# Half-empty taps of a 3x3 convolution as 64x64 quarters, in a fixed order with the neighbour layer in slots

## The chip, the cores and the metric

The kernel runs on one core of a Trainium2 chip. The engines that matter are TensorE (PE, matrix products), VectorE (DVE), ScalarE (ACT), GpSimd (POOL) and SyncE (SP, which here only issues DMAs). Each engine works through its own queue of instructions in order, and engines wait for each other by semaphores. DMAs are issued from a queue of SP or ACT, and an issue that has to wait holds what stands behind it in that queue. The metric is the device time of one execution in microseconds; fewer is better.

## The reference, cut to what matters

The network has four layers on an input `x` of 8 images, 64 channels, 128x128 pixels, in float32. Each layer adds its result to its input:

```python
x = x + _L0_conv_ref(_gn(x), ...)   # deformable convolution
x = x + _L1_conv_ref(_gn(x), L1_conv_weight)   # 3x3 convolution, 64 -> 64 channels, padding 1
x = x + _L2_conv_ref(_gn(x), ...)   # scans along rows and columns
x = x + _L3_conv_ref(_gn(x), ...)   # nearest neighbours ("neighbour layer"), see below
```

`_gn` is a group norm over pairs of channels of an image. Layer 1, the one that is changed, is a plain convolution:

```python
return jax.lax.conv_general_dilated(x, weight, window_strides=(1, 1),
    padding=[(PAD, PAD), (PAD, PAD)], dimension_numbers=('NCHW', 'OIHW', 'NCHW'))
```

Layer 3 shrinks the image by a 4x4 convolution with stride 4 to 32x32, looks for every pixel for the nine of its 7x7 surroundings that differ most, averages them, runs a second 3x3 convolution over both, scales by an attention value, and resizes to 128x128 bilinearly. Its pieces run beside layer 1.

## The kernel before, in words

**Layout.** Two images make a pair, so that 2 x 64 channels fill 128 partitions; there are four pairs. Layer 0 is done for all pairs first. `Net.rest` then takes the pairs one after the other: `conv3x3` (layer 1), `scan_layer` (layer 2), and `neighbours` (layer 3). `neighbours` is a generator: it is cut into pieces by `yield`, and the generator of pair p is handed as `aside` to the `conv3x3` of pair p+1, which draws pieces from it. Pair 0 has no pieces beside it; the pieces of pair 3 run alone at the end. Two large tiles in SBUF (`room`) change roles from pair to pair.

**The convolution** (`conv3x3`, from L603). Sixteen *fills* (L624 to L630) bring the normed image into the other room in a form for products with 128 rows of contraction: ACT norms 8 image rows into a tile `nx` (two buffers), and SP issues four DMAs that put even image rows on partitions 64 to 127 and odd image rows, moved by one, on partitions 0 to 63, for both images. At one position of this room a product thus reads two image rows that follow each other. A tap pair `m` covers two of the rows that an output row needs; the three kernel rows need two such pairs, and one of the two is half empty: for even output rows (`e` = 0) the pair `m` = 1 has weights on partitions 0 to 63 alone, for odd ones (`e` = 1) the pair `m` = 0 has them on 64 to 127 alone. The other halves of the weights are zeros (memset at L615). For 8 output rows (a *row block*) and each parity `e`, 12 products (3 shifts `dx`, 2 tap pairs `m`, 2 images `i`) go into one bank of PSUM: image 0 to partitions 0 to 63, image 1 to 64 to 127 (L632 to L641). As data are float32, each product is two matmul instructions in the program, the low and then the high part of the weights. VectorE adds the bank to the residual (L643), and takes statistics for the next norm (`bn_stats`, L647). The tag `b` has two buffers in PSUM.

**The neighbour layer's pieces**, 46 in number (from L976):
- one for weights and norm factors (`quarter`: loads from ACT's queue, L988 and L990, 32 tiny products, L996),
- eight for the 4x4 convolution (loads of 1 MB in four issues on ACT's queue, L1010, two blocks ahead; 32 instructions, L1018; ACT empties them, L1019),
- two for transposes, the write to DRAM (L1033) and the loads back (L1035, L1044),
- sixteen for distances and maxima (`farthest`, L1137 to L1153, one product and ten VectorE instructions; `means` of the piece before: transposes L1162, copy by ACT L1164, products L1167),
- two for the second 3x3 convolution (its weights loaded by SP, L1072, L1073; L1086, L1087),
- one for attention and a widened image (L1090 to L1103),
- sixteen for the upsampling, two for each of eight tiles: the first loads a tile of the residual by SP (`up_x`, two buffers, L1109) and interpolates along rows (ACT L1116, VectorE L1117), the second does eight additions on VectorE (L1125, L1126) and issues the store by SP (L1127).

**What sets the order.** In this region the framework's scheduler orders each engine's queue from its own estimate of when things are ready; program order is a priority. Pieces are drawn at three places per row block, one piece each. It can so move a load ahead of a store that stands before it in the program, or a piece's loads ahead of the convolution. The scan layers before and after are written in an order of their own (`manual_schedule`), which the scheduler leaves as it is.

Of the kernel before, what the change touches and what calls it, by code (L numbers as in the profile page):

```python
# [9 lines left out]
F32 = mybir.dt.float32  # L10
# [6 lines left out]
P = 128  # L17
C = 64
H = 128
# [23 lines left out]
class Net:  # L43
# [559 lines left out]
    def conv3x3(self, p, a, room, r, nb, aside):  # L603

        nc, src = self.nc, self.ins["l1_w"]
        st = self.small.tile([P, NCH, 6], F32, tag="st", name=f"gn2_st{p}")
        two = room.rearrange("p (i n w) -> p i n w", i=2, w=H)  # L610
        half = [slice(0, C), slice(C, P)]
        with self.tc.tile_pool(name=f"b_conv{p}", bufs=1) as cp, self.tc.tile_pool(name=f"b_conv2_{p}", bufs=2) as wp:

            w = cp.tile([P, 2, 2, 3, C], F32, name=f"l1_w{p}")
            nc.gpsimd.memset(w, 0.0)  # L615
            for e in range(2):
                for n in range(2):
                    for h in range(2):
                        dy = 2 * n - 1 + h - e
                        if abs(dy) < 2:  # L620
                            nc.scalar.dma_start(w[half[h], e, n], src[:, 3 * dy + 3 : 3 * dy + 6, :])
            nc.gpsimd.memset(two[half[0], :, 0, :], 0.0)
            nc.gpsimd.memset(two[half[1], :, H // 2, :], 0.0)
            for n in range(16):  # L624
                t = wp.tile([P, 2, 4, H], F32, tag="t", name=f"nx{p}_{n}")
                rows = a[:, 8 * n : 8 * n + 8, :].rearrange("p (m e) w -> p e m w", e=2)
                nc.scalar.activation(t, rows, AF.Identity, bias=nb, scale=r)
                for i in range(2):
                    nc.sync.dma_start(two[half[1], i, 4 * n : 4 * n + 4, :], t[half[i], 0])
                    nc.sync.dma_start(two[half[0], i, 4 * n + 1 : 4 * n + 5, :], t[half[i], 1])  # L630
            for n in range(0, H // 2, 4):
                for e in range(2):  # L632
                    po = self.ps.tile([P, 4, H], F32, tag="b", name=f"c1_{p}_{n}_{e}")
                    calls = []
                    for dx in (0, -1, 1):
                        c0, c1 = max(0, -dx), min(H, H - dx)
                        for m in range(2):
                            for i in range(2):
                                calls.append((po[half[i], :, c0:c1], w[:, e, m, dx + 1], two[:, i, n + m : n + m + 4, c0 + dx : c1 + dx]))
                    for k, (o, lt, mv) in enumerate(calls):  # L640
                        nc.tensor.matmul(o, lhsT=lt, rhs=mv, start=k < 2, stop=k >= len(calls) - 2)  # L641
                    rows = a[:, 2 * n : 2 * n + 8, :].rearrange("p (m e) w -> p e m w", e=2)[:, e]
                    nc.vector.tensor_add(rows, rows, po)  # L643
                    next(aside, None)
                for k in range(2):
                    g = n // 2 + k
                    nc.vector.bn_stats(st[:, g, :], a[:, 4 * g : 4 * g + 4, :].rearrange("p h w -> p (h w)"))  # L647
                next(aside, None)
            for _ in aside:
                pass  # L650
        return self.groupnorm(self.small, self.ps1, "small", st, "gn2")


# [517 lines left out]
class Scan:  # L1171
# [106 lines left out]
    def products(self, g, h, py, fx, xs, first):  # L1278

        om = self.outs.rearrange("p (n c) -> p n c", c=P)  # L1280
        calls = [(om[:, T + 1 + h - k], fx[:, :, k, :]) for k in (h, 1 - h)] if fx is not None else []
        calls += [(om[:, 2 * f + h], x) for f, x in xs]
        if py is None:
            py = self.net.ps.tile([P, 2, NB], F32, tag="y", name=self.name("py", h, g))
        for n, (lt, mv) in enumerate(calls):
            self.nc.tensor.matmul(py, lhsT=lt, rhs=mv, start=first and n == 0, stop=n == len(calls) - 1 and (fx is not None))  # L1286
        return py
# [387 lines left out]
```

## Time and profile before

| | us |
|---|---|
| median of 3 runs | 15756.33 (15753.49 to 15758.31) |
| the profiled execution | 15728.88, its span 15727.1 |
| convolution, pair 0: first fill to next stage's L1376 | 11733.0 to 11912.1 |
| pair 1, with pieces: the same | 12608.8 to 12889.9 |
| pair 2 | 13588.1 to 13869.5 |
| pair 3 | 14570.4 to 14852.4 |

Times within the execution count from the start of the span. An engine's busy time in a stretch says whether it is full there; matmuls overlap, so a PE that is busy throughout can still be loaded in steps of different length. A line such as `SPq` shows what an engine's queue issued and when; for DMAs it is the issue, not the transfer. `x3072` counts instructions, and the number behind the bar is the time in which at least one of the group ran.

### The profile page before, as it was taken

How to read it: one execution, taken by the hardware profiler on the slowest of the kernel's cores; microseconds unless marked ns; L12 is line 12 of the kernel's file. 1: busy time of each engine (PE TensorE's matmuls, PEld its weight loads, DVE VectorE, ACT ScalarE, POOL GpSimd, SP SyncE). 2: the span in 40 equal slices, each digit the busy share in tenths (PEclk: the TensorE clock that was granted, in tenths of full speed). 3: DMA queues.
4: the chain of work that ended last, by engine and by line, in shares of the span. 5: the costliest groups of instructions: out<-in, count | busy, mean ns of one | idle time of the engine just before them, and what ended most of it. 6: DMA issues, size and time to landing. Idle time of an engine off the chain costs nothing. (4 is left out here: it accounts for less than half of the span.)

```text
span 15727.1 us, 121681 instructions
## 1 busy us (share of the span) xinstructions
PE 10293.3 (65%) x32760; PEld 3736.6 (24%) x32760; DVE 11824.0 (75%) x27353; ACT 3233.2 (21%) x5498; POOL 10294.7 (65%) x10572
## 2 busy tenths in 40 slices
PE   7864577447755553776556655564338888888886
PEld 2211122112211111221111111111114444434443
DVE  6777777777777777777777777777766958779587
ACT  1100111001100000110000000000015637456373
POOL 5777777777777777777777777777753605336052
PEclk9986698669977775988778887787569999999998
DMA  5444444345533333543333333333342443534434
GB/s 174 125 122 134 131 149 155 115 121 157 156 118 117 115 115 111 157 138 120 113 116 115 115 120 115 115 115 108 108 141 71 122 120 98 133 117 123 118 92 114
DMA packets 901297, 1933.56 MB, mean 123 GB/s; under 512 B 200060, under 2 KB 436996, under 8 KB 877572
## 3 DMA queue, kind: packets, MB, share of 16 engines
q0 software_dynamic: 442368, 1208.55, 26.2%
q1 hardware_dynamic: 383200, 679.50, 14.2%
q10 hardware_dynamic: 75044, 37.72, 1.2%
q8 instruction: 265, 4.34, 0.1%
q14 instruction: 420, 3.44, 0.1%
HBM read 1540.74 MB, written 208.10 MB: 111 GB/s over the span
## 5 line engine op out<-in xcount | busy, mean ns | idle before, releaser
L380 POOL DMA_INDIRECT g<-table,idx x9216 | 8716.7, 946 | 2822.5 <-issue 2636.4
L391 DVE TENSOR_TENSOR g<-g,corner_weights 128x256 f32<-128x256 f32 x9216 | 3778.1, 416 | 2699.9 <-DMA g<-table,idx 2660.2
L392 DVE TENSOR_REDUCE sm<-g 128x64 f32<-128x256 f32 x9216 | 5016.9, 580 | 9.0
L292 PE MATMUL po<-xe,wt 128*54 128x512 f32 (+3 forms) x8384 | 4292.6, 627 | 13.6 <-ACT ob L302 13.0
L398 PE MATMUL sp<-ident,sm 128*128 128x128 f32 x4096 | 1536.4, 380 | 4169.7 <-DVE sm L392 4154.4
L403 ACT COPY s<-sp 128x512 f32<-128x512 f32 x1024 | 598.8, 585 | 8695.4 <-PE sp L398 8695.2
L398 PEld LDWEIGHTS sp<-ident,sm 128*128 128x128 f32 x4096 | 629.8, 155 | 6730.5 <-DVE sm L392 5062.0
L292 PEld LDWEIGHTS po<-xe,wt 128*54 128x54 f32 x8384 | 901.5, 132 | 1341.4 <-issue 1059.8
L409 PE MATMUL yp<-s,wd 128*64 128x512 f32 (+1 forms) x2560 | 903.2, 713 | 25.4 <-ACT s L403 24.8
L1433 POOL COPY l_yb<-ln_y 128x512 f32<-128x512 f32 x128 | 87.9, 718 | 1242.0 <-ACT room L1413 1128.0
L641 PE MATMUL c<-room,l_w 128*64 128x508 f32 (+1 forms) x3072 | 737.9, 605 | 43.1 <-DMA room<-nx 28.3
L1209 ACT ACTIVATE fx<-room,ln_b,ln_g 128x512 f32<-128x512 f32 x512 | 654.2, 1304 | 89.1 <-DMA in<-fx 80.1
L1225 PE MATMUL pv<-in,tabs 128*128 128x512 f32 x1024 | 555.4, 669 | 98.1 <-DMA in<-fx 47.0
L1286 PE MATMUL py<-in,outs 128*128 128x512 f32 x1024 | 520.3, 633 | 2.4 <-ACT ms L1313 2.4
L1286 PE MATMUL py<-x,outs 128*128 128x512 f32 x1024 | 476.2, 600 | 0.0
L1324 POOL TENSOR_TENSOR ms<-ms,ln_y 128x512 f32<-128x512 f32 x256 | 268.4, 1059 | 271.2 <-DVE ln_y L122 266.6
L1259 DVE TENSOR_TENSOR_SCAN z<-tabs,z,uu 128x256 f32<-128x256 f32 x512 | 407.5, 837 | 27.0 <-POOL uu L1475 26.3
L1303 PE MATMUL pc<-mix,h 64*128 64x128 f32 x4096 | 314.7, 295 | 138.2 <-DVE h L1568 96.5
L641 PEld LDWEIGHTS c<-room,l_w 128*64 128x64 f32 x3072 | 293.4, 139 | 377.1 <-issue 309.7
L402 PE MATMUL s<-ident,sm 128*64 128x128 f32 x512 | 176.3, 344 | 300.7 <-DVE sm L392 288.6
L643 DVE TENSOR_TENSOR room<-room,c 128x512 f32<-128x512 f32 x128 | 87.7, 687 | 371.9 <-PE c L641 368.7
L409 PEld LDWEIGHTS yp<-s,wd 128*64 128x64 f32 (+1 forms) x2560 | 261.6, 159 | 433.5 <-issue 317.9
(423 smaller groups left out, 10271.4 us busy)
## 6 DMA issues: line engine op xcount, KB each, us to landing
g<-table,idx POOLq DMA_INDIRECT x9216, 2.7
in<-fx SPq DMA_DIRECT2D x1024, 128.0 KB
xe<-in_x_dram SPq DMA_DIRECT2D x56, 1408.0 KB
table<-q SPq DMA_DIRECT2D x256, 256.0 KB
y<-ys SPq DMA_DIRECT2D x128, 256.0 KB
room<-in_x_dram SPq DMA_DIRECT2D x64, 512.0 KB
room<-nx SPq DMA_DIRECT2D x256, 128.0 KB
back<-z SPq DMA_DIRECT2D x128, 256.0 KB
```

The lines of the kernel that those rows point to most:

```text
L292: nc.tensor.matmul(po[:, r0:r1, c0:c1], lhsT=wt[:, t, :], rhs=xe[:, row + r0 : row + r1, c0 + dx : c1 + dx], start=n == 0, stop=n == len(u ...
L380: nc.gpsimd.indirect_dma_start(out=tq[:, k, :], out_offset=None, in_=flat[i], in_offset=bass.IndirectOffsetOnAxis(ap=idx[:, at : at + 1], ...
L391: nc.vector.tensor_mul(t[:, ks], t[:, ks], w)
L392: nc.vector.tensor_reduce(sm[:, ks], t[:, ks].rearrange("p k q c -> p k c q"), axis=mybir.AxisListType.X, op=ALU.add)
L398: nc.tensor.transpose(sp[:, j, :], sm[:, j * P : (j + 1) * P], self.ident)
L403: nc.scalar.copy(st[i][:, :, m * P : (m + 1) * P], sp)
L409: nc.tensor.matmul(yp[half[i], :], lhsT=wd[rows, j, :], rhs=src[rows, :], start=j == 0, stop=j == 4)
L641: nc.tensor.matmul(o, lhsT=lt, rhs=mv, start=k < 2, stop=k >= len(calls) - 2)
L1209: self.nc.scalar.activation(fx[:, e].rearrange("p h (o m) -> p h o m", m=self.INNER), src, AF.Identity, bias=self.w["ln1_b"], scale=self.w ...
L1225: self.nc.tensor.matmul(pv, lhsT=self.tabs[:, at : at + P], rhs=fx[:, :, h, :], start=h == 0, stop=h == 1)
L1259: self.nc.vector.tensor_tensor_scan(z[:, i, 1 : NB + 1], decay, u[:, i, :], z[:, i, 0:1], ALU.mult, ALU.add)
L1286: self.nc.tensor.matmul(py, lhsT=lt, rhs=mv, start=first and n == 0, stop=n == len(calls) - 1 and (fx is not None))
```

## The change

Three things change in `conv3x3`:

1. The products of half-empty tap pairs no longer read 128 partitions with zeros for weights on half of them. `quarters` reads the 64 partitions that have weights, so that each such product takes a 64x64 quarter of the array. The two parities' quarters of one `dx` are written one after the other: four products (parity 0 or 1, image 0 or 1) that use the four different quarters and two banks. The number of products stays 24 per row block.
2. The order is written out under `manual_schedule`: three fills first; then for each row block `k` the fill `k + 3`, the full products of parity 0, slot, the quarters of both parities, the add of parity 0, slot, the full products of parity 1, its add, the two statistics, slot.
3. Pieces of the neighbour layer are drawn in these 48 slots by a table (`due`): one piece in every second slot up to ten pieces in slot 19, then 36 pieces in the 26 slots from 20 to 45. Whatever a piece issues on any engine, its DMAs on SP and ACT too, keeps its place in program order.

```diff
-            for n in range(16):
+            def fill(n):
                 t = wp.tile([P, 2, 4, H], F32, tag="t", name=f"nx{p}_{n}")
 ...
-            for n in range(0, H // 2, 4):
-                for e in range(2):
-                    po = self.ps.tile([P, 4, H], F32, tag="b", name=f"c1_{p}_{n}_{e}")
 ...
-                        for m in range(2):
-                            for i in range(2):
-                                calls.append((po[half[i], :, c0:c1], w[:, e, m, dx + 1], two[:, i, n + m : n + m + 4, c0 + dx : c1 + dx]))
-                    for k, (o, lt, mv) in enumerate(calls):
-                        nc.tensor.matmul(o, lhsT=lt, rhs=mv, start=k < 2, stop=k >= len(calls) - 2)
 ...
+            def beside(slot):
+                due = (slot + 1) // 2 if slot < 20 else 10 + (slot - 19) * 36 // 26
+                while done[0] < due:
+                    done[0] += 1
                     next(aside, None)
+            def products(po, k, e, m, rows, left):
+                for dx in (0, -1, 1):
+                    c0, c1 = max(0, -dx), min(H, H - dx)
+                    left[e] -= 1
+                    for i in range(2):
+                        mv = two[rows, i, 4 * k + m : 4 * k + m + 4, c0 + dx : c1 + dx]
+                        nc.tensor.matmul(po[e][half[i], :, c0:c1], lhsT=w[rows, e, m, dx + 1], rhs=mv, start=left[e] == 5, stop=left[e] == 0)
+            def quarters(po, k, left):
+                for dx in (0, -1, 1):
+                    c0, c1 = max(0, -dx), min(H, H - dx)
+                    for e in range(2):
+                        left[e] -= 1
+                        for i in range(2):
+                            mv = two[half[e], i, 4 * k + 1 - e : 4 * k + 5 - e, c0 + dx : c1 + dx]
+                            nc.tensor.matmul(po[e][half[i], :, c0:c1], lhsT=w[half[e], e, 1 - e, dx + 1], rhs=mv, start=left[e] == 5, stop=left[e] == 0)
 ...
+            with self.tc.manual_schedule():
+                for n in range(3):
+                    fill(n)
+                for k in range(16):
+                    if k + 3 < 16:
+                        fill(k + 3)
+                    po = [self.ps.tile([P, 4, H], F32, tag="b", name=f"c1_{p}_{k}_{e}") for e in range(2)]
+                    left = [6, 6]
+                    products(po, k, 0, 0, slice(0, P), left)
+                    beside(3 * k)
+                    quarters(po, k, left)
+                    add(po, k, 0)
+                    beside(3 * k + 1)
+                    products(po, k, 1, 1, slice(0, P), left)
+                    add(po, k, 1)
+                    for g in (2 * k, 2 * k + 1):
+                        nc.vector.bn_stats(st[:, g, :], a[:, 4 * g : 4 * g + 4, :].rearrange("p h w -> p (h w)"))
+                    beside(3 * k + 2)
+                for _ in aside:
+                    pass
```

More of the change, by code (lines that the diff above doesn't have):

```diff
@@ L630, in conv3x3 @@
                     nc.sync.dma_start(two[half[0], i, 4 * n + 1 : 4 * n + 5, :], t[half[i], 1])
-            for n in range(0, H // 2, 4):
-                for e in range(2):
-                    po = self.ps.tile([P, 4, H], F32, tag="b", name=f"c1_{p}_{n}_{e}")
-                    calls = []
-                    for dx in (0, -1, 1):
-                        c0, c1 = max(0, -dx), min(H, H - dx)
-                        for m in range(2):
-                            for i in range(2):
-                                calls.append((po[half[i], :, c0:c1], w[:, e, m, dx + 1], two[:, i, n + m : n + m + 4, c0 + dx : c1 + dx]))
-                    for k, (o, lt, mv) in enumerate(calls):
-                        nc.tensor.matmul(o, lhsT=lt, rhs=mv, start=k < 2, stop=k >= len(calls) - 2)
-                    rows = a[:, 2 * n : 2 * n + 8, :].rearrange("p (m e) w -> p e m w", e=2)[:, e]
-                    nc.vector.tensor_add(rows, rows, po)
-                    next(aside, None)
[L645 to L648, printed above, removed]
@@ L649, in conv3x3 @@
-            for _ in aside:
-                pass
+            done = [0]
+            def beside(slot):
+                due = (slot + 1) // 2 if slot < 20 else 10 + (slot - 19) * 36 // 26
+                while done[0] < due:
+                    done[0] += 1
+                    next(aside, None)
+            def products(po, k, e, m, rows, left):
[5 more added lines that the diff above has]
+                        nc.tensor.matmul(po[e][half[i], :, c0:c1], lhsT=w[rows, e, m, dx + 1], rhs=mv, start=left[e] == 5, stop=left[e] == 0)
@@ new lines, in add @@
+            def add(po, k, e):
+                rows = a[:, 8 * k : 8 * k + 8, :].rearrange("p (m e) w -> p e m w", e=2)[:, e]
+                nc.vector.tensor_add(rows, rows, po[e])
+            with self.tc.manual_schedule():
[18 more added lines that the diff above has]
+                    pass
```

## The prediction

> **What bounds the kernel now.** I read the page first (shares, the convolution's group), then busy time by stage, then the convolution's own line by stage, then SyncE's queue in the last of the stages. The page says that no engine is full over the whole span, and that the 3x3 convolution (L641) has 3072 matmul instructions:
>
> ```profile
> span 15727.1 us, 121681 instructions
> ...
> PE 10293.3 (65%) x32760; PEld 3736.6 (24%) x32760; DVE 11824.0 (75%) x27353; ACT 3233.2 (21%) x5498; POOL 10294.7 (65%) x10572
> ...
> L641 PE MATMUL c<-room,l_w 128*64 128x508 f32 (+1 forms) x3072 | 737.9, 605 | 43.1 <-DMA room<-nx 28.3
> ```
>
> The source has 1536 products, so one product is two instructions. The four convolutions lie at 11733 to 11912 us (pair 0, alone), and, with the neighbour layer of the pair before beside them, at 12609, 13588 and 14570 us, 281, 281 and 282 us each from their first fill (ACT, L627) to the next stage's first instruction (L1376). Busy time by stretch, with columns stretch, its length, PE, PEld, DVE, ACT, POOL, granted clock, DMA share and GB/s:
>
> ```profile
> 11733.00:11912.10 179.10, 167.75 (x773) 90.88 (x774) 46.39 (x83) 19.73 (x16) 0.00 (x0) 0.97 0.21 51
> 12608.80:12699.50 90.70, 82.92 (x500) 48.89 (x501) 12.98 (x28) 22.35 (x24) 0.00 (x0) 0.90 0.84 177
> 12699.50:12716.90 17.40, 17.40 (x81) 5.62 (x78) 5.95 (x9) 3.56 (x4) 0.00 (x0) 1.00 0.56 133
> 12716.90:12795.00 78.10, 78.10 (x374) 35.33 (x374) 61.77 (x179) 11.56 (x32) 0.00 (x0) 1.00 0.00 1
> 12795.00:12823.00 28.00, 27.64 (x133) 10.36 (x131) 5.78 (x15) 5.25 (x13) 0.00 (x0) 1.00 0.25 91
> 12823.00:12885.90 62.90, 50.02 (x228) 17.56 (x224) 62.03 (x119) 9.31 (x26) 0.00 (x0) 0.94 0.57 217
> ```
>
> Row one is pair 0: TensorE full, everything else idle. The others are pair 1's stages: the 4x4 convolution (L1018), its hand-over through DRAM, the distances and maxima (L1137 to L1167), the second 3x3 convolution (L1086), and the upsampling (L1117 to L1127). TensorE is full without a hole through all of them but the last, where VectorE is (62.03 of 62.90). So a cheaper convolution pays until 12823, and not after. The convolution's own instructions in pair 0 and in the last stage:
>
> ```profile
> 11733.00:11912.10 179.10, 166.77 (x768) 90.06 (x768) 0.97 0.21 51
> ...
> 12823.00:12885.90 62.90, 48.85 (x224) 16.55 (x220) 0.94 0.57 217
> ```
>
> SyncE's queue in the upsampling, before:
>
> ```profile
> 12814.42 0.80 SPq L1109 DMA_DIRECT2D up_x<-y  x2
> 12828.32 0.34 SPq L1127 DMA_DIRECT2D out_dram<-up_x  x1
> 12832.17 0.32 SPq L1109 DMA_DIRECT2D up_x<-y  x1
> 12835.13 0.34 SPq L1127 DMA_DIRECT2D out_dram<-up_x  x1
> 12839.26 0.32 SPq L1109 DMA_DIRECT2D up_x<-y  x1
> 12843.70 0.34 SPq L1127 DMA_DIRECT2D out_dram<-up_x  x1
> ```
>
> Two loads go out first. Every load is one tile ahead of the store before it, so VectorE never waits for one: stores are 6.8 to 8.7 us apart.
>
> **The change, part by part.** The sum goes against the profiled execution (15728.9 us, span 15727.1); the median of the runs is 27.4 above it, and I add the difference to the median.
>
> *Quarters.* In steady state single starts in the trace come in pairs, one for each column half, a pair every 0.426 us (11800.071, .497, .923). A row block of 8 image rows has 48 instructions, 24 pairs, 10.2 us. After, 24 instructions stay in pairs (12 x 0.426 = 5.12) and 24 become 64x64 tiles. Four of these at once never run in this trace. Two at once is the upper end: 5.12 us, no gain. Four at once is the lower end: 6 x 0.426 = 2.56; less is excluded, since each quarter of the array still streams its 6. The nearest rows are 64x64 products at 5101.629 and 5101.636 (opposite corners, both running) and the row halves of L1303 (13136.000 and .007). Each pair there starts together though the second half of an earlier product is still to come, so I take four.
>
> The row on order: where one bank of pair 0 ends, the instruction that signals VectorE starts at 11801.446, and the first of the next bank, behind it in the program, at 11801.349. The Trainium skill, "TensorE: Matmul & The Clock Gate", section "The mechanism" of Part 3, speaks against the change: matmuls start and end in program order. As each product is two passes on one tile, strict order would let only neighbours overlap, two at a time, the quarters would gain nothing (5.12), and the total would be the last rival's. The trace contradicts it here by those 97 ns.
>
> Changing the tile shape: before the 64x64 products of L409 the step is 0.52 in place of 0.43, and the next 0.48, so 0.15 us per change, 0.30 per row block. A row block is 5.12 + 2.56 + 0.30 = 7.98 us, or three slots of 2.66.
>
> *Pair 0* runs no pieces. Before: 11737.7 to 11904.5, 166.8 us. After: 3.0 (the wait for fills at its start: 166.8 - 384 x 0.4265) + 48 x 2.66 = 130.7. **-36.1 us.** The adds hide: VectorE has 2 x 0.69 + 2 x 0.69 of work in 8. Fills run ahead on ACT, one in 2.6 us against 8 needed.
>
> *The fixed order, pairs 1 to 3.* Now each queue runs as written. From the first fill, pair 1:
> - First product 5.8 (as before, 12614.5). Slots 0 to 17: 18 x 2.66 = 47.9. Eight blocks of L1018 at 3.6 (64 instructions took 7.63 less the last one's tail) = 28.8; L996 1.4.
> - Before, weights and the first loads of the neighbour layer were issued from 12594, ahead of the fills. Now they stand in ACT's queue behind four fills: pair 0's fills end at +9.4, then 8 issues of 0.6, landing about 2 later: +16.3, where TensorE comes at +12.6. A wait of 3.7, with the products of the slot queued behind it. Twelve load issues of 0.65 follow; the first 1 MB lands near +24: 1.4 more, and 1.5 for a cold start. L1018 ends at **90.5**; before, 90.7.
> - Last block to first distance: 12699.95 to 12716.87, 16.9, plus 0.5: **107.9**. Four slots and two transposes cover 12.1 of it; 5.3 is a hole.
> - Distances: TensorE per piece 0.75 (L1137), 0.64 to the copy, 0.53 of copy (L1164), 0.65 (L1167): 2.57, x16 = 41.1. Before, convolution products filled the copy's 0.53; in a fixed order nothing does. 11 slots 29.3. Five slots hold two pieces, whose transposes wait for VectorE's chain of about 3.3 us: 1.1 each, 5.5. **183.8** (before, 186.0 at the load of L1086's weights).
> - Weights of L1086: issue, landing, subtract (12794.8 to 12799.3): 4.4, now bare. Two halves of 7.5, slot 33, then two slots, attention, add, statistics and the first interpolation 9.6: **215.4**; before, 214.2.
>
> So everything the quarters save there (12 row blocks against 11.3, at 2.2 each, some 26 us) goes into holes that the old order did not have.
>
> *Upsampling.* Each piece pair is load, interpolate, then add, store. As written on SyncE that is load 0, store 0, load 1: load 1 stands behind a store that waits for VectorE to finish tile 0. VectorE then lacks tile 1 until store and load, 2 MB, have passed. The two loads at 12814.42 (2 MB) moved until 12820.9: 6.4 us. Lower end: a load alone, 3.9; upper, store and load in turn, 3.9 + 4.85 (the chain's last load) = 8.7. I take 6.4, the same bytes. Interpolation (2.0) and the convolution's VectorE work hide in it. Eight additions are 4.83, so a cycle is 11.3 against some 8.3 before: 7 x 11.3 + 4.83 = 83.9, plus 2.0 for the last fill's four DMAs between store 0 and load 1. 85.9 against 62.9: **+23.0**.
>
> *End.* Two adds and two statistics now come after the last addition: 2.4, then the norm, 5.5 (pair 0: 11906.6 to 11912.1). Before, this lay beside the last store: 4.0. **+3.9.**
>
> Pair: 215.4 + 85.9 + 7.9 = 309.2 against 281.1: +28.1. Three: +84.3. With pair 0: **+48.2**: 15777 for the profiled execution, **15805** for the median.
>
> **The rivals.**
> - *Not slower: the load is not late.* If x tiles land within VectorE's other work, the upsampling stays at 62.9: 3 x -23.0, net -21, 15735. For it: DMA is only 0.57 busy there, 6.4 is from two reads, not a write and a read. Against it: the queue's order. It decides where a cycle falls under 9.0 us (21 cycles, each 48.2 / 21 = 2.3 less).
> - *The holes stay closed.* 3.7 + 1.4 + 5.3 + 16 x 0.53 + 5.5 + 4.4 = 28.8 per pair. Without them 48 - 86 = -38: 15718. For: TensorE runs a little ahead in the row above. Against: instructions that wait for another engine hold the queue. Break-even at 16 us per pair.
> - *The quarters do nothing:* two at once. Pair 0 loses 41, and each other pair about 26 (12 x 2.56, part of it in holes): 48 + 41 + 78 = 167, 15923.
>
> **How the numbers follow.** 0.2% (31 us) is about what a measurement here can tell from no change. Forecast 0.62, late load absent 0.17, holes closed 0.08, both of these 0.05 (near 15650), quarters idle 0.08. The forecast's own range is 15765 to 15850 (cycle 9.9 to 12.5, holes 10 either way). From it 0.50 is slower and 0.12 same; the late load absent gives 0.11 same, 0.06 faster; holes closed 0.03 and 0.05; both, faster; idle quarters, slower. Slower 0.58, same 0.26, faster 0.16. The range runs from just under the closed holes' 15718 to 15870, leaving out the idle quarters, both together and tails.
>
> **What would show it.** Right: pair 0 from 179 to about 143 us; four matmuls starting in each 0.43 us during quarters; SyncE's issues in the upsampling strictly load, store, load; VectorE at about 70% there, idle before L1125 with a DMA as releaser; the upsampling near 86 us while its start stays within 10 us. Wrong: upsampling near 63 us, or its start more than 15 us earlier, or 5 us per set of quarters.

## The result and the profile after

The changed kernel takes 15909.23 us (median of 4 runs, 15906.5 to 15914.74) against 15757.32 us (15753.49 to 15759.02) before: ratio 1.0097, 95% interval 1.008 to 1.0115. It is 152 us slower. The forecast was 15805, 48 us slower, with a range up to 15870: the direction was right, the size was a third of what came.

The time is best read in four windows, one for each pair: from the convolution's first fill (ScalarE, L627 before, L629 after) to the next stage's first VectorE instruction (L1376, L1411). Everything else is the same in both traces but for some 3 us in the scans, and for layer 0, which no edit touches and which took 30 us longer in the profiled run of after than in that of before; the medians do not hold these 30 us. In the changed kernel's line numbers L650 are the full products, L660 the quarters, L664 the adds, L1053 the 4x4 convolution, L1172 the distances, L1121 the second 3x3 convolution, L1144 the residual's load, L1160 and L1161 the additions, L1162 the store.

| us | pair 0 | pair 1 | pair 2 | pair 3 | sum |
|---|---|---|---|---|---|
| before | 179.0 | 281.2 | 281.4 | 282.0 | 1023.6 |
| after | 143.6 | 341.8 | 343.2 | 342.4 | 1171.0 |
| forecast of after | 142.9 | 309.3 | 309.5 | 310.1 | 1071.8 |

Pair 0 gained 35.4 us (forecast 36.1). Each of the others lost 61 us (forecast 28). The page of the changed kernel has no engine fuller than before over the whole span; of the convolution it lists the full products, half as many instructions as L641 had:

```profile
span 15908.1 us, 121658 instructions
...
PE 10231.8 (64%) x32760; PEld 3630.8 (23%) x32760; DVE 11870.1 (75%) x27353; ACT 3233.1 (20%) x5498; POOL 10322.1 (65%) x10572
...
L650 PE MATMUL c<-room,l_w 128*64 128x508 f32 (+1 forms) x1536 | 401.3, 652 | 68.0 <-DVE room L664 42.3
```

The idle time before them was 43.1 us before, mostly ended by a load; now it is 68.0, mostly ended by VectorE's add. Busy time by stretch in the changed kernel, first pair 0, then the stages of pair 1: to the end of the 4x4 convolution, its hand-over, the distances to the last key, the second 3x3 convolution and attention, the upsampling from first to last addition, the tail. The columns are stretch, length, PE, PEld, DVE, ACT, POOL, granted clock, DMA share, GB/s:

```profile
11763.20:11906.80 143.60, 132.28 (x773) 41.07 (x774) 46.37 (x83) 19.71 (x16) 0.00 (x0) 0.95 0.27 63
12607.50:12698.70 91.20, 83.68 (x574) 40.59 (x576) 18.32 (x36) 13.80 (x16) 0.00 (x0) 0.92 0.79 148
12698.70:12718.80 20.10, 12.40 (x74) 4.17 (x71) 1.29 (x2) 3.56 (x4) 0.00 (x0) 0.91 0.57 141
12718.80:12805.60 86.80, 67.73 (x338) 31.23 (x338) 73.01 (x182) 17.04 (x36) 0.00 (x0) 0.89 0.11 25
12805.60:12843.40 37.80, 31.45 (x156) 10.70 (x160) 6.47 (x17) 7.19 (x14) 0.00 (x0) 0.84 0.19 55
12843.40:12941.20 97.80, 45.28 (x172) 11.49 (x164) 60.29 (x106) 9.88 (x29) 0.00 (x0) 0.70 0.44 156
12941.20:12949.30 8.10, 1.17 (x4) 1.00 (x4) 6.15 (x23) 0.00 (x0) 0.00 (x0) 0.50 0.53 202
```

The first row has TensorE full: the quarters work there. In the first row of pair 1 TensorE idles 7.5 us, about as before (82.92 of 90.70 us busy). In the rows behind it no engine is full. TensorE idles 7.7 us in the hand-over and 19.1 us beside the distances, where it was full at clock 1.00 before; the mean clock there is 0.89 to 0.91. The upsampling holds the largest loss, 98 us against 63, with VectorE's work as before (60 us).

SyncE's queue in that upsampling:

```profile
12877.14 0.34 SPq L1162 DMA_DIRECT2D out_dram<-up_x  x1
12877.57 0.38 SPq L1144 DMA_DIRECT2D up_x<-y  x1
12889.99 0.34 SPq L1162 DMA_DIRECT2D out_dram<-up_x  x1
12890.42 0.38 SPq L1144 DMA_DIRECT2D up_x<-y  x1
```

And VectorE's first and last addition of the tile between them, from its order of time:

```profile
12884.56 0.69 DVE L1160 SCALAR_TENSOR_TENSOR up_x<-up,up_x 128x512 f32<-128x512 f32 x1 [5.24 <-DMA up_x<-y]
...
12889.27 0.69 DVE L1161 SCALAR_TENSOR_TENSOR up_x<-up,up_x 128x512 f32<-128x512 f32 x1
```

Every load stands behind the store of the tile before it. From the load's issue to the first addition 7.0 us pass, the eight additions take 5.4, the store's and the load's issue 0.4: a cycle of 12.8 us.

TensorE at the hand-over, in order of time (in brackets the idle time before, and what ended it):

```profile
12708.32 2.78 PE L650 MATMUL c<-room,l_w 128*64 128x512 f32 x12
12718.81 1.19 PE L1172 MATMUL d<-xs,cat 128*128 128x256 f32 x2 [7.71 <-ACT xs L1080]
12719.93 5.81 PE L660 MATMUL c<-room,l_w 64*64 64x512 f32 x24
...
12733.29 3.85 PE L650 MATMUL c<-room,l_w 128*64 128x512 f32 x11
...
12745.41 2.79 PE L660 MATMUL c<-room,l_w 64*64 64x512 f32 x24
```

The hole is followed by a set of quarters at half speed (5.81 us; the last line shows a set of the same kind at 2.79), and 13 us later steps are slow again (3.85 for what takes 2.72 a set later). The prediction had priced holes by their idle time, with one cold start of 1.5 us at the beginning. The second slow set is in pair 1 alone; in pairs 2 and 3 the distances take 85.1 us in place of 86.8.

The second 3x3 convolution starts behind a hole too, and its first half (36 instructions) takes longer than its second:

```profile
12812.65 10.00 PE L1121 MATMUL pf<-cat,l_w 128*64 128x512 f32 x36 [4.57 <-DVE l_w L1109]
...
12825.04 7.57 PE L1121 MATMUL pf<-cat,l_w 128*64 128x512 f32 x36
```

### The profile page after: what moved, and what is told of

Its sections match the earlier page's. It is cut to its first block, busy times and chain, and to the rows that moved or that the text cites. A ratio compares the mean times of both kernels' runs of the same rounds, so it can differ in the third digit from the quotient of the medians.

```text
span 15908.1 us, 121658 instructions
## 1 busy us (share of the span) xinstructions
PE 10231.8 (64%) x32760; PEld 3630.8 (23%) x32760; DVE 11870.1 (75%) x27353; ACT 3233.1 (20%) x5498; POOL 10322.1 (65%) x10572
## 5 line engine op out<-in xcount | busy, mean ns | idle before, releaser
L650 PE MATMUL c<-room,l_w 128*64 128x508 f32 (+1 forms) x1536 | 401.3, 652 | 68.0 <-DVE room L664 42.3
L664 DVE TENSOR_TENSOR room<-room,c 128x512 f32<-128x512 f32 x128 | 87.5, 686 | 410.0 <-PE c L660 305.6
L402 PE MATMUL s<-ident,sm 128*64 128x128 f32 x512 | 176.3, 344 | 299.1 <-DVE sm L392 289.0
L400 PE MATMUL s<-ident,sm 128*64 128x128 f32 x1024 | 282.8, 368 | 125.2 <-DVE sm L392 123.2
```

What stands on the lines that cost most here:

```text
L650: nc.tensor.matmul(po[e][half[i], :, c0:c1], lhsT=w[rows, e, m, dx + 1], rhs=mv, start=left[e] == 5, stop=left[e] == 0)
```

## The experiments

Nine of the runs were made on chips on which layer 0 takes 14.8 to 15.0 ms in place of 11.7 and varies from run to run by more than most edits are worth; so they are read by the four windows of the profiled execution. Windows in which nothing was changed show how far these scatter: pairs 1 to 3 of e5 are within 1.6 us of the changed kernel's and those of e8 within 4.7, and pair 0 of e11 is 3.4 us longer than that of the kernel before. A difference of 5 us in one window is therefore not clear. Two theories run through them. **A**: the quarters gain wherever TensorE is full; what costs is the fixed order, by a load behind a store, by holes, and by the clock behind the holes. **B**: the quarters themselves cost where the neighbour layer runs beside them. All windows:

| us | pair 0 | pair 1 | pair 2 | pair 3 | sum |
|---|---|---|---|---|---|
| e1 fixed order, full products | 178.7 | 365.4 | 361.8 | 363.8 | 1269.7 |
| e2 scheduler's order, quarters | 143.1 | 278.7 | 278.4 | 279.3 | 979.5 |
| e3 after, load ahead | 143.1 | 305.3 | 307.0 | 305.0 | 1060.4 |
| e5 after, holes in pair 0 | 159.3 | 343.4 | 343.2 | 342.0 | 1187.9 |
| e6 after, weights early | 143.7 | 342.5 | 340.9 | 339.9 | 1167.0 |
| e7 mended order | 142.9 | 313.5 | 314.4 | 315.7 | 1086.5 |
| e8 after, orders of quarters in pair 0 | 157.8 | 345.6 | 342.8 | 347.1 | 1193.3 |
| e9 e2, weights early | 143.2 | 269.1 | 271.9 | 272.0 | 956.2 |
| e10 e7, mended again | 143.2 | 283.7 | 284.2 | 283.6 | 994.7 |
| e11 before, weights early | 182.4 | 279.1 | 279.7 | 279.5 | 1020.7 |
| e12 e9, weights behind xs | 142.9 | 275.0 | 275.3 | 271.9 | 965.1 |
| e13 e10, half convolution ahead | 143.6 | 282.8 | 283.1 | 282.4 | 991.9 |

### e1: the order without the quarters

```diff
-    mv = two[half[e], i, 4 * k + 1 - e : 4 * k + 5 - e, c0 + dx : c1 + dx]
-    nc.tensor.matmul(..., lhsT=w[half[e], e, 1 - e, dx + 1], ...)
+    mv = two[:, i, 4 * k + 1 - e : 4 * k + 5 - e, c0 + dx : c1 + dx]
+    nc.tensor.matmul(..., lhsT=w[:, e, 1 - e, dx + 1], ...)
```

(`...` stands for what is left out of a line or between lines.)

> Changed kernel, but the half-empty products read all 128 partitions again (zeros for weights on one half); order and slots stay. Theory A (the quarters gain wherever TensorE is full, and the fixed order is what costs): pair 0 goes back to about 179 us from 143.6; in pairs 1 to 3 the six quarter sets beside the 4x4 convolution cost 2.4 us more each, those beside the distances some, those in the upsampling nothing: +20 to +30 a pair. In all +95 to +125: 16005 to 16035. Theory B (the quarters themselves cost beside the neighbour layer: changes of tile shape, or a lower clock): pairs 1 to 3 get shorter than 342, and the total is at or under 15909.

Pair 0 went back to 178.7 and the others rose by 21 us each, to 364 on average: 99 us in all, at the low end of A's interval. B falls. In pair 1 (24 us more) they lie where A puts them: 11 up to the end of the 4x4 convolution, 8 from there to the last key, 2 up to the first addition, 2 in the upsampling.

### e2: the quarters without the order

```diff
-            with self.tc.manual_schedule():
-                for n in range(3):
-                    fill(n)
+            for n in range(16):
+                fill(n)
 ...
-                    beside(3 * k)
+                next(aside, None)
 ...
```

> Quarters as in the changed kernel, but no order of their own: the scheduler orders the queues, pieces at three places per row block as before. Theory A (the fixed order costs, the quarters gain): pair 0 about 144; pairs 1 to 3 at most the 281 of before, down to 266 where TensorE was full beside the distances (78 us there, VectorE only 62 busy): 15677 to 15722, faster than before. Theory B (quarters cost beside other work): pairs 1 to 3 over 290, total over 15750.

Ratio to the kernel before 0.9977 (0.9963 to 0.9992), the windows 44 us shorter. A holds, at the poor end of its interval: pair 0 gained 36 us, the other pairs 3 each, which is within the scatter. A quarter set that gains 2.2 us in pair 0 gained almost nothing there. TensorE beside the distances shows why:

```profile
15870.48 1.07 PE L660 MATMUL c<-room,l_w 64*64 64x512 f32 x2
...
15871.96 1.07 PE L660 MATMUL c<-room,l_w 64*64 64x512 f32 x4
...
15874.60 1.94 PE L660 MATMUL c<-room,l_w 64*64 64x508 f32 x12
```

The scheduler cuts the sets into bites and puts them between the pieces. A bite of two instructions (one product) takes about 1.0 us to the next line's start, one of four also 1.0, one of twelve 1.9; a whole set of 24 takes 2.72. A product alone has no other quarter to share its time with: twice 0.43 us, and 0.15 for the change of shape. In bites of one or two products quarters are no faster than what they replaced. The convolution's instructions beside pair 1's distances, first in the kernel before, then in e2 (instructions, time in which one of them ran):

```profile
L641 PE MATMUL c<-room,l_w 128*64 128x508 f32 (+1 forms) x194 | 51.6, 604 | 0.0
...
L650 PE MATMUL c<-room,l_w 128*64 128x508 f32 (+1 forms) x92 | 28.8, 606 | 0.0
L660 PE MATMUL c<-room,l_w 64*64 64x508 f32 (+1 forms) x96 | 23.8, 608 | 0.0
```

TensorE is full there at clock 1.00 in both, and 188 instructions, half of them quarters, take about as long as 194 full ones did. What e2 gained lies elsewhere in the window.

### e3: the load ahead of the store

```diff
-                    x = wp.tile([P, 4, 4, H], F32, tag="x", name=f"up_x{p}_{n}")
 ...
-                    nc.sync.dma_start(xf, self.y[p][:, s])
+                    for m in ((0, 1) if n == 0 else (n + 1,)):
+                        if m < 8:
+                            x = wp.tile([P, 4, 4, H], F32, tag="x", name=f"up_x{p}_{m}")
+                            xs.append(x)
+                            nc.sync.dma_start(x.rearrange("p h f w -> p (h f w)"), self.y[p][:, m * 2048 : (m + 1) * 2048])
 ...
```

> Changed kernel with the residual's load of tile n+1 issued ahead of the store of tile n in the upsampling, as the scheduler had it. Theory A (the late load is the upsampling's cost): the cycle falls from 12.8 to 8 to 9 us, VectorE is full there, the stage from first addition to last goes from 98 to 62 to 70 us: -28 to -35 a pair, 15805 to 15825. Rival (a load takes as long beside a store, so that transfers set the cycle): the cycle stays over 11 us, 15870 or more.

Pairs 1 to 3 fell to 305 to 307, 37 us less each, a little more than was expected of A. From first to last addition it is now 62 us. The stage's row, and SyncE's queue in it:

```profile
16072.90:16134.70 61.80, 39.15 (x172) 10.16 (x164) 59.91 (x106) 9.94 (x29) 0.00 (x0) 0.84 0.61 230
```

```profile
16091.31 0.32 SPq L1147 DMA_DIRECT2D up_x<-y  x1
16094.95 0.34 SPq L1167 DMA_DIRECT2D out_dram<-up_x  x1
16099.26 0.32 SPq L1147 DMA_DIRECT2D up_x<-y  x1
...
16106.57 0.32 SPq L1147 DMA_DIRECT2D up_x<-y  x1
```

VectorE is full again (59.91 of 61.80) and the cycle is 7.3 to 8.0 us. Three fifths of a pair's loss were this one load; the rival, that transfers set the cycle anyway, falls.

### e5: what a hole costs, by itself

In pair 0, where nothing else runs, TensorE waits after seven row blocks for VectorE copies.

```diff
+                    late = {1: 3, 3: 4, 5: 5, 7: 6, 9: 8, 11: 10, 13: 14}.get(k, 0) if p == 0 else 0
 ...
+                        for _ in range(late):
+                            nc.vector.tensor_copy(pause, a[:, 8 * k : 8 * k + 4, :])
                     products(po, k, 1, 1, slice(0, P), left)
 ...
+                        nc.tensor.matmul(tiny[0:C], lhsT=pause[:, 0, 0:C], rhs=pause[:, 0, 0:1], start=True, stop=True)
```

> Changed kernel; in pair 0, where nothing but the convolution runs, TensorE is made to wait at seven places for VectorE copies: holes of about 0.5, 1.2, 1.9, 2.6, 4, 5.4 and 8 us, some 24 us in all. Clock theory (a hole lowers the granted clock and the products behind it run at half speed for some us): steps of 0.85 us in place of 0.43 behind the longer holes, pair 0 takes 178 to 190 us in place of 143.6. Rival (the 0.85 us steps in pairs 1 to 3 come from other engines' traffic): steps stay at 0.43 us, pair 0 about 167 us.

The small product L687 reads what VectorE copies, and the full products of the next row block stand behind it. The holes came out shorter than meant: five of 0.44, 0.90, 1.83, 2.75 and 4.60 us, 10.5 in all, so pair 0 took 159.3 and not 178 or more. Neither number was met, but the steps decide:

```profile
15003.71 0.28 PE L687 MATMUL tiny<-pause 128*64 128x1 f32 x2 [1.83 <-DVE pause L683]
15003.82 2.78 PE L650 MATMUL c<-room,l_w 128*64 128x512 f32 x12
...
15022.78 0.27 PE L687 MATMUL tiny<-pause 128*64 128x1 f32 x1 [2.75 <-DVE pause L683]
...
15023.02 4.30 PE L650 MATMUL c<-room,l_w 128*64 128x512 f32 x11
...
15045.35 0.27 PE L687 MATMUL tiny<-pause 128*64 128x1 f32 x1 [4.60 <-DVE pause L683]
...
15045.59 4.96 PE L650 MATMUL c<-room,l_w 128*64 128x512 f32 x11
```

The granted clock (the column before the DMA share) beside the first set, beside the slow and the full steps of the second, and beside the end of the last hole and the slow steps behind it:

```profile
15003.80:15006.50 2.70, 2.70 (x14) 0.78 (x14) 1.94 (x3) 0.00 (x0) 0.00 (x0) 1.00 0.02 6
15022.80:15026.10 3.30, 3.30 (x10) 1.48 (x12) 1.98 (x3) 0.00 (x0) 0.00 (x0) 0.50 0.02 5
15026.20:15027.20 1.00, 1.00 (x6) 0.19 (x2) 0.00 (x0) 0.00 (x0) 0.00 (x0) 1.00 0.00 0
15043.30:15050.00 6.70, 4.65 (x14) 1.83 (x14) 3.83 (x8) 0.00 (x0) 0.00 (x0) 0.50 0.00 0
```

Up to 1.83 us a hole costs its length alone here. Behind 2.75 us the clock is 0.50 for 3.4 us and the set takes 1.6 us more; behind 4.60 us it is 0.50 to 15050.0 and the set takes 2.2 more. VectorE works as long beside the slow steps of the second set (1.98 us) as beside the full ones of the first (1.94), and DMA is at most 0.02, so this is the clock and not traffic: the rival falls. The Trainium skill, "TensorE: Matmul & The Clock Gate", Part 1, says that the array falls to half its rate after an idle window of about 3.4 us and comes back after about as long of work. The run agrees in kind, but the fall comes earlier: the clock drops 2.7 us after the start of the fourth hole and 2.5 us after that of the fifth. Full steps are back 3.4 and 4.7 us into the work.

### e6: the weights of the second 3x3 convolution early

```diff
+            nc.sync.dma_start(w1, ins["l3_w1"])
+            nc.sync.dma_start(w2, ins["l3_w1"][C:P])
             nc.sync.dma_start(kept, x1f)
 ...
+                nc.vector.tensor_sub(w1[half[0]], w1[half[0]], w2)
                 late = None
 ...
```

> Changed kernel with the weights of the second 3x3 convolution (w1, w2) loaded and subtracted before the distances, into memory of their own. In the changed kernel TensorE stands still for 4.6 us ahead of that convolution, and its first half then takes 9.8 us in place of 7.5. From the last key to the first addition of the upsampling it is 37.8 us there. If a hole costs only its idle time: 33 to 34 us. If it costs idle time and then half speed: 30.5 to 32 us, the first half at 7.5.

From the last key to the first addition it is 31.6 us (31.6, 31.6, 32.0), the number of "idle and half speed", but not by that way: the first product of the convolution comes 1.1 us behind the last key in place of 7.0, while its first half takes 9.1 us, hardly less than 9.8. A wait of 3.45 us for the last key still stands ahead of it, and the clock is 0.50 in the first 3.4 us of that half. And the 6 us were given back: the two loads stand on SyncE ahead of the store of x1, and the first distance comes 2 to 4 us later. Pairs gained 1.4 us on average, which is within the scatter. As a price of a hole this run is inconclusive.

### e8: the order in which quarters are issued

```diff
+                orders = [
+                    [(dx, e, i) for dx in (0, -1, 1) for e in range(2) for i in range(2)],
+                    [(dx, e, i) for dx in (0, -1, 1) for i in range(2) for e in range(2)],
+                    [(dx, e, i) for e in range(2) for dx in (0, -1, 1) for i in range(2)],
+                    [(dx, e, i) for e in range(2) for i in range(2) for dx in (0, -1, 1)],
+                ]
+                for dx, e, i in orders[k // 4 if p == 0 else 0]:
 ...
```

> Changed kernel; in pair 0 the twelve quarter products of a set are issued in four orders, four row blocks each: shift, parity, image (as it is); shift, image, parity; parity, shift, image; parity, image, shift. If a waiting product starts as soon as its quarter is free, whatever stands ahead of it in the queue, every order takes 2.7 us a set. If only products that stand next to each other overlap, the third order takes about 5.2 us a set, two quarters at a time, and the fourth up to 10.

One set of each order, from TensorE's order of time:

```profile
14935.84 2.79 PE L663 MATMUL c<-room,l_w 64*64 64x512 f32 x24
...
14967.83 2.79 PE L663 MATMUL c<-room,l_w 64*64 64x512 f32 x24
...
14999.82 3.70 PE L663 MATMUL c<-room,l_w 64*64 64x512 f32 x24
...
15035.44 5.52 PE L663 MATMUL c<-room,l_w 64*64 64x512 f32 x24
```

The first two orders take 2.72 us to the next line's start, the third 3.63, the fourth 5.45 (each alike in its four row blocks). Neither expectation holds alone. TensorE does start waiting products out of turn, or the third order would take 5.2 and the fourth up to 10; but it doesn't see past everything that waits. How far it looks can't be told from four orders. The Trainium skill, "TensorE: Matmul & The Clock Gate", section "The mechanism" of Part 3, has matmuls start in program order. By the two estimates just named, 5.2 and up to 10 us, the third and fourth order measure less than that would allow, so here the measurement decides; a queue that is worked through in order is not what TensorE shows for these products.

### e7 and e10: the fixed order mended

e7 takes e3's loads and e6's early weights, adds one slot later in VectorE's queue, and a new table of slots with six sets in the hand-over.

```diff
-                due = (slot + 1) // 2 if slot < 20 else 10 + (slot - 19) * 36 // 26
+                due = (slot + 1) // 2 if slot < 17 else table[slot - 17]
 ...
-                    add(po, k, 0)
                     beside(3 * k + 1)
+                    add(po, k, 0)
 ...
```

> Changed kernel's fixed order with its waits taken out: residual loaded a tile ahead, weights of the second 3x3 convolution early, the adds one slot later in VectorE's queue, and a slot table that puts six sets of products between the 4x4 convolution and the first distance (four before). Theory A (holes, the clock behind them, and the late load are all that the fixed order costs): pairs 1 to 3 come down from 342 to 275 to 290 us, pair 0 stays at 144. Rival (an order of this kind has a further cost, as adds that wait or the loss of the small fills between pieces): over 300 us.

It missed: 313 to 316. The upsampling held (65 us), but the first distance came 129 us after the first fill, 18 later than in the changed kernel. The hand-over, in order of time over all engines:

```profile
15786.61 1.25 SPq L1086 DMA_DIRECT2D xs<-x  x2
15796.01 1.91 ACT L1087 ACTIVATE xs<-xs 64x2048 f32<-64x2048 f32 x1 [15.54 <-DMA xs<-x]
15797.94 0.60 ACT L1096 ACTIVATE sq<-xt 128x512 f32<-128x512 f32 x1
...
15798.57 0.69 DVE L1097 TENSOR_REDUCE own<-sq 128x8 f32<-128x512 f32 x1 [17.23 <-ACT sq L1096]
15799.17 0.68 DVE L665 TENSOR_TENSOR room<-room,c 128x512 f32<-128x512 f32 x1
...
15800.00 5.36 PE L661 MATMUL c<-room,l_w 64*64 64x512 f32 x20 [15.14 <-DVE room L665]
```

A chain over three queues: ScalarE's square of xs waits for a load; the squares of xt stand behind it; VectorE's reduction waits for those; the convolution's add stands behind that; and TensorE waits for the bank that the add empties. Six sets were there to cover the load, and a wait on another engine kept them out. In e10 the square of xs stands behind the squares of xt, the weights' loads behind those of xs, and one set beside each distance:

```diff
-                nc.scalar.activation(xs[half[1]], xs[half[1]], AF.Square)
+                nc.sync.dma_start(w1, ins["l3_w1"])
+                nc.sync.dma_start(w2, ins["l3_w1"][C:P])
 ...
+                nc.scalar.activation(xs[half[1]], xs[half[1]], AF.Square)
                 late = None
```

> The mended fixed order once more, with what held TensorE 15 us ahead of the distances in the first try taken away: ScalarE's square of xs, which waits for a load, stands behind the squares that VectorE waits for and no longer ahead of them; w1 and w2 are loaded behind xs; the slot table puts one set of products beside every distance (one beside every two before). If the chain load, ScalarE, VectorE, PSUM bank, TensorE made the hole: first distance at 106 to 110 us after the first fill (129 in the first try), and with 16 distances at 5.3 us (one set and one piece without a wait for a key) the pairs come to 281 to 295 us, against 281 before. If the hole has another cause, the first distance stays over 120 us.

First distance at 108.2 to 108.7 us, pairs 283.6 to 284.2: as expected of the chain. Its hand-over, and its distances to the last key:

```profile
12669.30:12686.60 17.30, 17.30 (x105) 5.64 (x105) 7.88 (x12) 5.81 (x6) 0.00 (x0) 1.00 0.81 203
12686.60:12768.30 81.70, 71.98 (x410) 32.85 (x410) 72.44 (x182) 17.13 (x35) 0.00 (x0) 1.00 0.16 37
```

TensorE is full in the hand-over, and the clock is 1.00 in both rows (0.91 and 0.89 in the changed kernel). The waits that are left are nearly all for ScalarE's copy: beside each distance TensorE idles 0.5 to 0.6 us for it, 9.7 us together. With the others taken out, the fixed order (with quarters and early weights) is 2 us a pair longer than the kernel before, no more than the scatter, and not 61. In its only run it took 15685.7 us, beside 15743.22 of the kernel before on that chip; 16 us of this lie behind the last scan, where pair 3's neighbour layer runs alone and gains mostly by the early weights.

### e9, e11, e12, e13: towards a faster version

e9 is e2 with e6's edit; e11 is the kernel before with the same edit; e12 is e9 with the weights' loads behind those of xs (of e10's diff the two loads alone); e13 is e10 with the first half of the second 3x3 convolution issued ahead of the last transposes:

```diff
+                second(0)
                 yield
                 self.means(wp, *late)
```

> Quarters in the scheduler's order (the run before that beat the kernel before), and the weights of the second 3x3 convolution loaded before the distances. There 8.1 us pass between the last key and the first product of that convolution, 4 of them for the weights. If the chain of the neighbour layer sets the end: 3 to 5 us less a pair, pairs at 274 to 276 us, some 55 us under the kernel before in all. Rival (the products of the convolution that are left over set the end): pairs stay at 278 to 279.

> The kernel before, full products in the scheduler's order, with w1 and w2 loaded before the distances and nothing else changed. With quarters the same edit took pairs from 279 to 271 us. If that gain belongs to the weights alone: pairs here 271 to 276 in place of 281 to 282, 15 to 30 us less in all, pair 0 at 179. If it needs the quarters (TensorE full without them): pairs stay over 279.

> Quarters in the scheduler's order, w1 and w2 loaded before the distances but behind xs. In the run with them ahead of xs the first distance came 17.9 us after the 4x4 convolution, against 16 without the early weights. If the chain of the neighbour layer sets the end: 1 to 3 us less a pair than 269 to 272, in all about 70 us under the kernel before. If not: the same as that run, about 66 under.

> The mended fixed order, and the first half of the second 3x3 convolution issued ahead of the last transposes, so that its 7.5 us run while VectorE makes the last keys (in the mended order TensorE had 4.4 us between the last key and that convolution, both halves behind it). From the last key to the first addition 28 us become some 21: pairs at 276 to 279 in place of 284, pair 0 at 143, and 70 to 85 us less than the kernel before in all. If VectorE bounds what follows (its work in the upsampling, 57 us, and one more set of adds): 280 to 283, 55 to 65 us less.

e9: pairs 269 to 272, 8 us under e2, more than the 3 to 5 expected of the chain: with its weights there in time, the scheduler starts the second 3x3 convolution 6.3 us ahead of the end of the last key, and in e2 it started 8.1 us behind it. Ratio 0.9962 (0.9947 to 0.9978). e11: pairs 279.1 to 279.7, the second number, so without quarters the early weights are worth 2 us a pair, within the scatter; ratio 0.9987 (0.9978 to 0.9997), of which 12 us lie behind the last scan. Put the other way, with early weights the quarters in the scheduler's order are worth 8 us a pair (e9 beside e11), where e2 had 3. e12: its windows are 9 us longer than e9's, not shorter; beside pair 1's distances it takes 73.4 us where e9 takes 69.2, and the cause of that stays open. Ratio 0.9954 (0.994 to 0.9967), 15669.74 us against 15743.22. The intervals of e9 and e12 overlap. Both beat both kernels: quarters in the scheduler's order, with the weights early. e13: 282.8, the second number for the pairs, though by the ratio it is only some 36 us under the kernel before (55 to 65 expected): the half convolution starts as the last key ends (both at 190.5 us), since the last distance, transposes and a set of products stand ahead of it on TensorE, which goes from these to it without a gap. Ratio 0.9981 (0.9969 to 0.9993).

## Why the prediction was right and wrong

By its own steps, for pair 1 (times from the first fill):

| step | forecast | measured |
|---|---|---|
| pair 0, whole window | 142.9 | 143.6 |
| end of the 4x4 convolution | 90.5 | 91.7 (the row above is cut at 91.2) |
| first distance | 107.9 | 111.3 |
| distances to last key | 75.9 | 86.8 |
| last key to first addition | 31.6 | 37.8 |
| upsampling | 85.9 | 97.8 |
| tail | 7.9 | 8.1 |

- **Quarters: right.** Four at a time, 2.72 us a set with 0.16 us for the change of shape; a row block 5.27 + 2.72 = 7.99 us (forecast 7.98). The rival "two at once" falls. The row of 97 ns that this rested on was read rightly, but the cause is narrower than "waiting products run ahead": e8 shows that four at a time holds for two of four orders. That the kernel's order is one of them was not worked out, and is luck in that part.
- **The load behind the store: right in mechanism, too small.** 11.3 us a cycle was forecast, 12.8 came. The load took 7.0 us to the first addition (6.4 taken), the eight additions 5.4 (4.83 taken), and two issues 0.4 (not counted). Seven times 1.5 are 10.7 of the 11.9 us missing per pair.
- **Holes: right in their place, priced too low.** This is the step that failed. The prediction put a hole at its idle time, put that too short, and put the half-speed steps behind it at nothing, but for one cold start of 1.5 us per pair. Beside the distances TensorE idled 19.1 us (14.0 forecast) and was busy 67.7 where the forecast had 61.9: 5.8 us. The half-speed steps shown above make 3.0 of them in the set of quarters and 1.1 in the later set. The hand-over's hole was 7.7 us, 5.3 forecast. Between last key and first addition the first half of the 3x3 convolution took 9.8 us for 7.5, and it started 7.0 us behind the last key, where 4.4 had been put. Together 20.5 of the 32.6 us missing per pair. That waits are what made most of them is shown by e10: its hand-over has no hole, the clock is 1.00 from there to the first addition, and this comes at 218 us in place of 236. It changes several things at once and keeps the waits for ScalarE's copy, so how the 20.5 divide between idleness and clock is read from the rows above and not shown by a run of its own.
- **The sum.** Per pair 3.4 + 10.9 + 6.2 + 11.9 + 0.2 = 32.6 us were missing, 98 over three pairs; the windows rose by 147 where 48 was forecast.
- **The rivals.** "Load not late" and "holes closed" were wrong of this kernel. The first is right of e3, and e10 is close to both: its load is not late and its holes are closed but for the waits for ScalarE's copy, which the prediction had put at 16 x 0.53 and which took 9.7 us. Both together had been put near 15650, some 106 us under the kernel before; the windows of e10 are 29 us under it.

## What to carry to other kernels

Under an order written by hand, follow every wait through all queues, not only the one in which it stands: a load behind a store cost 37 us a pair here, and a square of one tile kept products of another layer out by way of three engines. Price a hole in front of TensorE by its length and by the slow steps behind it, and ask whether the gaps after it let the clock recover. A product that is cheaper only beside its partners has to be issued with them: in whole sets the quarters paid 35 us in pair 0 and 21 us in each other pair (e1), cut into bites by the scheduler 3 us in each of these, no more than the scatter (e2), and 8 where the weights came early (e9 beside e11).

## What was not expected of the hardware

- The granted clock is 0.50 or 1.00 in every trace of this case, and its low stretches last 3.41 us or whole multiples of it; a value between, such as 0.89, is a mean over both.
- In pair 1 the clock behind the hole at the hand-over was 0.50 to 12725.3, 1.00 to 12728.7 and 0.50 again to 12735.5, though the waits in between were only 0.46 to 1.02 us long. In pairs 2 and 3 there is no second low stretch there. All three pairs show a further one of 3.4 us some 50 us into the distances, with no wait over 1.31 us just ahead of it (12769.7 to 12773.1 in pair 1). So the edge seen in e5, between 1.8 and 2.75 us, holds for a TensorE that is full around the hole, and not where several short waits follow each other. e10 waits 0.5 to 0.6 us beside each distance and keeps 1.00.
- The order of quarter products decides how many run at a time: 2.72, 2.72, 3.63 and 5.45 us for the same 24 instructions.
- A quarter product alone costs as much as two side by side, 1.0 us with the change of shape (e2).
